# Unread identity products on TensorE ahead of expected waits, in a float32 macaron block of six layers

## The chip, the cores and the metric

The kernel runs on one core of a Trainium2 chip. The metric is the device time of one execution in microseconds (us); the time of a kernel is the median of its runs.

## The reference, cut to what is computed

The input x has 8 batches of 512 tokens with 256 features. Six residual layers follow one another, each on the layer-normalised x. All arithmetic is float32.

```
x = x + 0.5 * fp4_ffn(layernorm(x), w_gate, w_up, w_down)        # hidden 704
x = x + retention(layernorm(x), Wv, Wk, bk, Wq, bq, Wo)          # decay 0.99, blocks of 128
x = x + 0.5 * fp4_ffn(layernorm(x), w_gate, w_up, w_down)
x = x + 0.5 * soft_moe(layernorm(x), gamma_x, gamma_slot, slot_embeds, w1, w2)
x = x + causal_attention(layernorm(x), q, k, v, o with LoRA)     # 16 heads of 16
x = x + 0.5 * soft_moe(layernorm(x), the same weights)

fp4_linear(x, w):  round x and w to FP4 in blocks of 16 along the features, then x @ w.T
soft_moe(x):  logits = rms(x) . rms(slot_embeds)                 # 1024 slots
              slots  = softmax over 8 experts, transposed, @ x
              out    = softmax over slots @ (gelu(slots @ w1) @ w2)    # hidden 1024
```

## The kernel before, in words

All weights stay in SBUF. Two batches are in work at a time, and the instructions of all of them are written into one static program, in an order that the build computes. Three lanes offer work: `front` (the first FFN, retention, the second FFN and the dispatch of the first mixture, lines 1322 to 1330), `back` (attention and the dispatch of the second mixture, lines 1332 to 1338) and `experts` (the expert products and the mixing back, lines 934 to 983). A lane is a generator; it yields the PSUM banks and the results that its next step needs. `drive` (line 1283) picks the lane whose step can begin now and that has had the least of TensorE. DVE steps that can be put off (normalising, rounding to FP4) are kept in chains and put in where DVE would stand (`put_off`, `fill`).

What decides is a model of time, the class `Meter` (line 70). Every instruction goes through `emit` (line 125), which finds when it can begin (`begins`, line 113: the engine is free, the operands are written, the bank has been read), adds a price (`cost`, line 163), records the end, and then issues the real instruction at line 149. That is why nearly all rows of the profile bear L149: they are told apart by tile names. The meter prices a float32 product of n columns at 1.67 ns a column, at least 0.107 us, and a transpose of 128 columns at 0.11 us (lines 167 to 179). A DMA is over after 0.1 us for the meter (line 165), and it knows no clock of TensorE.

PSUM is handed out by `take` as three pairs of banks and two single banks. `not_before` tells the meter when a bank was last read.

The steps that the change and the prediction touch, with their tiles:

- `ffn_weights` (line 513): the gate and up weights come by DMA in three parts, DVE rounds each to FP4, TensorE transposes it (`gut`, line 540), ACT copies it to `w_in`.
- `other_weights` (line 544): transposes `tr_wv`, products `wvo` (4 of 256 columns, lines 584 to 592), transposes `dnt` of the down weights, products `lora_q`, `lora_k`, `lora_v`, `lora_o` on small tiles that come by DMA into one buffer each, transposes `se` of the slot embeddings.
- `ffn` (line 660): for each of four token tiles a transpose `tr_f` of the rounded rows, two times four products `gu_f` of 352 columns, silu and product to `h_f`, rounding, six transposes `hTp_f`, six products `dn_f`.
- `retention` (line 736): transposes `tr_r`, products `k_r`, `q_r`, `v_r`, `a_r` and `y_r`.
- `dispatch` (line 813): transposes `tr_m`, logits `lt_m`, transposes `sm_m`, `l_m` and `nm_m` around the two softmaxes, slots `sl_m` and their transposes `slT_m`.
- `experts`: products `h_e`, `p_e` and `mo_e`.
- `attention` (line 992): `qk_a`, `s_a`, `mx_a`, `st_a`, `c_a`, `ct_a`, `o_a`.

Of the kernel before, what the change touches and what calls it, by code (L numbers as in the profile page):

```python
# [69 lines left out]
class Meter:  # L70
# [2 lines left out]

    LOADS = {AF.Exp: "exp", AF.Gelu: "gelu", AF.Silu: "silu", AF.Sigmoid: "sigmoid"}
    HOP = 0.12
    HOLE = 0.3

    def __init__(self, nc):
        self._nc = nc
        self.at = dict.fromkeys(("PE", "DVE", "ACT", "POOL", "SP"), 0.0)  # L80
        self._written, self._used = {}, {}
        self._table, self._mode = None, None
        self.end, self.last = 0.0, None

        self.banks = set()

        self.holds = {"DVE": [], "POOL": []}

        self.kept, self.fill = None, None
        self.tensor = _Engine(self, "PE", nc.tensor)  # L90
        self.vector = _Engine(self, "DVE", nc.vector)
        self.scalar = _Engine(self, "ACT", nc.scalar)
        self.gpsimd = _Engine(self, "POOL", nc.gpsimd)
        self.sync = _Engine(self, "SP", nc.sync)
# [18 lines left out]
    def begins(self, engine, aps):  # L113

        at = self.at[engine]
        for x in aps:
            for k in self._pieces(x):
                who, t = self._written.get(k, (engine, 0.0))
                at = max(at, t if who == engine else t + self.HOP)
        for k in self._pieces(aps[0]):  # L120
            who, t = self._used.get(k, (engine, 0.0))
            at = max(at, t if who == engine else t + self.HOP)
        return at

    def emit(self, engine, op, call, args, kwargs):
        aps = [x for x in (*args, *kwargs.values()) if isinstance(x, bass.AP)]
        if engine == "DVE" and self.fill:

            while self.begins(engine, aps) > self.at[engine] + self.HOLE and self.fill():
                pass  # L130
        at, cost = self.begins(engine, aps), self.cost(engine, op, args, kwargs, aps)
        if self.shares(engine, op, aps):

            other = self.holds["POOL" if engine == "DVE" else "DVE"]
            for a, b in sorted(other):
                if a < at + cost and at < b:
                    at = b
            other[:] = [x for x in other if x[1] > at - 20.0]
            self.holds[engine].append((at, at + cost))
        at += cost  # L140
        self.at[engine] = self.end = at
        self.last = engine
        for k in self._pieces(aps[0]):
            self._written[k] = (engine, at)
        for x in aps:
            for k in self._pieces(x):
                self._used[k] = (engine, at)
            self._used[x.tensor.name] = at
        call(*args, **kwargs)  # L149

    def shares(self, engine, op, aps):
        if engine == "DVE":
            ins = sum(x.tensor.name not in self.banks for x in aps[1:])
            return ins > 1 or (op == "tensor_scalar" and self.banks.isdisjoint(x.tensor.name for x in aps))
        return engine == "POOL" and len(aps) > 1

    def flush(self):

        kept, self.kept = self.kept, None
        for x in kept or ():  # L160
            self.emit(*x)
# [84 lines left out]
def macaron(ctx: ExitStack, tc: tile.TileContext, a: dict, out: bass.AP):  # L246
    nc = Meter(tc.nc)
# [79 lines left out]

    ident = const.tile([P, P], FP, tag="ident", name="ident")
    make_identity(tc.nc, ident)

    identb = const.tile([P, P], BF, tag="identb", name="identb")
    nc.vector.tensor_copy(identb, ident)
# [3 lines left out]
    for t, step, cm in ((causalb, -1, 1), (causalTb, 1, -1)):  # L336
        nc.gpsimd.memset(t, 0.0)
        nc.gpsimd.affine_select(
            out=t, in_=t, pattern=[[0, 2], [step, P]], compare_op=ALU.is_ge, fill=-1e30, base=0, channel_multiplier=cm
# [851 lines left out]
    def go(lane, chain):  # L1191
# [4 lines left out]
        step()  # L1196
        chain.ready = nc.end + (nc.HOP if nc.last != "DVE" else 0.0)
        if token:
# [47 lines left out]
    def begins(lane):  # L1246
# [8 lines left out]
        for t in lane.needs:  # L1255
            if t not in done:
                return None
            at = max(at, done[t])
        return at + nc.HOP

# [22 lines left out]
    def drive(until=lambda: False):  # L1283
        while not until():
            live = [lane for lane in lanes if advance(lane)]
            if not live and not any(lane.later for lane in lanes):
                break
            least = min((lane.spent for lane in live), default=0.0)
            for lane in lanes:
                lane.spent = max(lane.spent, least - 30.0) if lane in live else max(lane.spent, least)  # L1290
            now = nc.at["PE"]
            if nc.at["DVE"] <= now + 0.5:
                found = put_off(max(now, nc.at["DVE"]))
                if found:
                    go(*found)
                    continue
            when = {lane.name: begins(lane) for lane in live}
            able = [lane for lane in live if when[lane.name] is not None]
            ready = [lane for lane in able if when[lane.name] <= now + SLACK]
            if ready:  # L1300
                emit(min(ready, key=lambda lane: lane.spent))
                continue
            first = min((when[lane.name] for lane in able), default=float("inf"))
            found = put_off(max(nc.at["DVE"], min(first, min(
                (c.ready for lane in lanes for c in lane.later), default=first))))
            if found and not (able and first <= nc.at["DVE"]):
                go(*found)
            else:
                assert able, [(lane.name, lane.banks, lane.needs) for lane in live]
                emit(min(able, key=lambda lane: when[lane.name]))  # L1310
# [94 lines left out]
```

## Time and profile before

| what | value |
|---|---|
| median of 3 runs | 3105.65 us (3105.08 to 10973.31) |
| profiled execution, its own time | 3104.87 us |
| span from first to last instruction | 3103.0 us |
| mean granted clock of TensorE | 0.985 |
| DVE busy | 1558.1 us (50%) |
| ACT busy | 1122.1 us (36%) |
| chain that ended last | PE 90%, DVE 6%, ACT 3%, issue 1% |

The span is what the profile shows; the execution's own time is 1.9 us longer, and its median neighbour another 0.8 us. "PE" is TensorE's matmuls (a transpose is one too), "PEld" its weight loads, which run beside the matmuls. A row of the timeline gives a start, the time from there to the end of the last of the merged instructions, the tiles and the number of records; in brackets stands the time that the engine sat idle before it and who ended that. Since matmuls are pipelined, the pace of a group is read from its start to the start of the next group, not from the duration of one.

### The profile page before, as it was taken

How to read it: one execution, taken by the hardware profiler on the slowest of the kernel's cores; microseconds unless marked ns; L12 is line 12 of the kernel's file. 1: busy time of each engine (PE TensorE's matmuls, PEld its weight loads, DVE VectorE, ACT ScalarE, POOL GpSimd, SP SyncE). 2: the span in 40 equal slices, each digit the busy share in tenths (PEclk: the TensorE clock that was granted, in tenths of full speed). 3: DMA queues.
4: the chain of work that ended last, by engine and by line, in shares of the span. 5: the costliest groups of instructions: out<-in, count | busy, mean ns of one | idle time of the engine just before them, and what ended most of it. 6: DMA issues, size and time to landing. Idle time of an engine off the chain costs nothing.

```text
span 3103.0 us, 36791 instructions
## 1 busy us (share of the span) xinstructions
PE 2948.5 (95%) x15342; PEld 2165.9 (70%) x15342; DVE 1558.1 (50%) x3533; ACT 1122.1 (36%) x1429; POOL 130.0 (4%) x231
## 2 busy tenths in 40 slices
PE   3778899999999999999999999999999999999999
PEld 2455677667776668666786677766777666776778
DVE  6775663645455454635646347354555543424240
ACT  2222352434424334434334343342442433443421
POOL 0000000000000000000000000000000000000000
PEclk8889999999999999999999999999999999999999
DMA  3000000000000000000000000000000000000000
GB/s 123 4 1 1 1 1 1 1 1 1 1 1 1 14 1 1 1 1 15 1 1 1 1 14 1 1 1 1 14 1 1 1 8 1 1 1 1 8 8 7
DMA packets 16806, 18.42 MB, mean 6 GB/s; under 512 B 2048, under 2 KB 16128, under 8 KB 16640
## 3 DMA queue, kind: packets, MB, share of 16 engines
q1 hardware_dynamic: 16640, 16.07, 1.6%
q8 instruction: 121, 1.98, 0.3%
q14 instruction: 45, 0.37, 0.0%
HBM read 11.87 MB, written 4.19 MB: 5 GB/s over the span
## 4 chain that ended last, share of the span: by engine, by line
PE 90%; DVE 6%; ACT 3%; issue 1%; DMA 0%; POOL 0%; SPq 0%; ACTq 0%; POOLq 0%; DVEq 0%
PE p_e L149 14%; PE h_e L149 14%; PE gu_f L149 10%; PE sl_m L149 7%; PE lt_m L149 7%; PE mo_e L149 7%; PE dn_f L149 5%; PE st_a L149 4%; PE s_a L149 4%; PE c_a L149 2%; PE qk_a L149 2%; PE l_m L149 1%; PE hTp_f L149 1%; PE a_r L149 1%; PE y_r L149 1%; PE k_r L149 1%
## 5 line engine op out<-in xcount | busy, mean ns | idle before, releaser
L149 PE MATMUL h_e<-slT_m,w1g 128*128 128x256 f32 x2048 | 463.5, 380 | 2.7 <-ACT pT_a L149 2.5
L149 PE MATMUL p_e<-w,hid_e 128*128 128x256 f32 x2048 | 456.5, 381 | 0.9 <-DVE x L149 0.9
L149 PEld LDWEIGHTS p_e<-w,hid_e 128*128 128x128 f32 x2048 | 388.0, 191 | 58.4 <-issue 4.6
L149 PEld LDWEIGHTS h_e<-slT_m,w1g 128*128 128x128 f32 x2048 | 381.7, 190 | 55.8 <-ACT pT_a L149 3.2
L149 PE MATMUL gu_f<-w_in,y_ffn 128*128 128x352 f32 x1024 | 333.3, 478 | 13.8 <-ACT y_ffn L149 8.3
L149 ACT ACT_TABLE_LOAD x222 | 284.8, 1283 | 109.9 <-PE h_e L149 59.1
L149 DVE TENSOR_REDUCE nmx<-s_a 128x2 f32<-128x256 f32 (+3 forms) x256 | 195.9, 818 | 187.3 <-PE s_a L149 187.0
L149 PEld LDWEIGHTS gu_f<-w_in,y_ffn 128*128 128x128 f32 x1024 | 198.4, 197 | 127.4 <-issue 18.8
L149 ACT ACTIVATE pT_a<-st_a 128x1024 f32<-128x1024 f32 (+1 forms) x192 | 158.8, 879 | 214.4 <-PE st_a L149 214.0
L149 PE MATMUL mo_e<-proc_e,lg_m 128*128 128x257 f32 x1024 | 233.2, 381 | 2.0 <-DVE x L149 1.7
L149 PE MATMUL sl_m<-y_dis,ed_m 128*128 128x257 f32 x1024 | 234.8, 383 | 0.0
L149 PE MATMUL lt_m<-yT_m,seT 128*128 128x512 f32 x512 | 231.5, 599 | 1.7 <-ACT yT_m L149 1.2
L149 ACT ACTIVATE hid_e<-h_e 128x1024 f32<-128x1024 f32 x128 | 131.1, 1024 | 242.2 <-PE h_e L149 241.9
L149 PEld LDWEIGHTS mo_e<-proc_e,lg_m 128*128 128x128 f32 x1024 | 190.5, 189 | 32.2 <-DVE x L149 2.9
L149 PEld LDWEIGHTS sl_m<-y_dis,ed_m 128*128 128x128 f32 x1024 | 192.9, 192 | 28.7 <-issue 1.9
L149 DVE TENSOR_SCALAR_CACHE_REDUCE lg_m<-lt_m 128x512 f32<-128x512 f32 x128 | 84.8, 688 | 222.1 <-PE lt_m L149 222.1
L149 PE MATMUL dn_f<-w_dn,hT_f 128*128 128x256 f32 x768 | 177.1, 383 | 0.0
L149 PEld LDWEIGHTS lt_m<-yT_m,seT 128*128 128x128 f32 x512 | 96.1, 192 | 105.5 <-issue 99.1
L149 ACT COPY proc_e<-p_e 128x512 f32<-128x512 f32 x64 | 37.6, 587 | 359.5 <-PE p_e L149 359.5
L149 PEld LDWEIGHTS dn_f<-w_dn,hT_f 128*128 128x128 f32 x768 | 143.8, 192 | 20.6 <-issue 2.8
L149 ACT ACTIVATE h_f<-gu_f 128x352 f32<-128x352 f32 x128 | 59.3, 464 | 271.6 <-PE gu_f L149 271.3
L149 DVE TENSOR_TENSOR h_f<-h_f,gu_f 128x352 f32<-128x352 f32 x128 | 66.5, 520 | 177.2 <-ACT h_f L149 176.9
(197 smaller groups left out, 3474.4 us busy)
## 6 DMA issues: line engine op xcount, KB each, us to landing
x<-in_L_attn_x SPq DMA_DIRECT2D x8, 512.0 KB, 4.1
out<-x SPq DMA_DIRECT2D x8, 512.0 KB, 3.0
w1g<-in_L_ffn_w SPq DMA_DIRECT2D x1, 1024.0 KB, 5.1
se<-in_L_ffn_slot_embeds SPq DMA_DIRECT2D x1, 1024.0 KB, 7.6
w<-in_L_ffn_w SPq DMA_DIRECT2D x1, 1024.0 KB, 10.1
dn<-in_L_ffn_w_down SPq DMA_DIRECT2D x1, 704.0 KB, 9.5
gu<-in_L_ffn_w_gate SPq DMA_DIRECT2D x1, 640.0 KB, 4.9
gu<-in_L_ffn_w_up SPq DMA_DIRECT2D x1, 640.0 KB, 7.0
```

Source lines behind the costliest of these rows:

```text
L149: call(*args, **kwargs)
```

## The change: what it does

In `emit`, just before a TensorE instruction is accounted for, a new method `keep_up` compares the time at which the instruction begins by the meter with the time from which TensorE is free and the bank that it writes has been read. If the difference is at least 1.0 us (`STAND`), and the output is two-dimensional with 128 partitions, it issues float32 products of the 128x128 identity with itself into the first up to 128 columns of that output. Their number is the difference less 0.3 us, divided by 0.11 us, or by 0.3 us as long as TensorE has had nothing to do by the meter. They are issued on the engine directly, not through the meter, so no other instruction's time in the meter changes. The instruction that follows writes the same columns anew. `macaron` hands the identity to the meter once it is made.

```
     HOP = 0.12
+    STAND = 1.0
     HOLE = 0.3
...
+        self.ident = None
...
         at, cost = self.begins(engine, aps), self.cost(engine, op, args, kwargs, aps)
+        if engine == "PE":
+            self.keep_up(at, aps[0])
...
+    def keep_up(self, until, out):
+        since = max([self.at["PE"]] + [self._used.get(k, (None, 0.0))[1] + self.HOP for k in self._pieces(out)])
+        if self.ident is None or until - since < self.STAND or len(out.shape) != 2 or out.shape[0] != 128:
+            return
+        n = min(128, out.shape[1])
+        took = 0.11 if self.at["PE"] else 0.3
+        for _ in range(int((until - since - 0.3 * self.STAND) / took)):
+            self._nc.tensor.matmul(out[:, :n], self.ident, self.ident[:, :n], start=True, stop=True)
...
     make_identity(tc.nc, ident)
+    nc.ident = ident
```

In the program that results, the order on DVE, ACT, POOL and the DMA queues is that of before, and so is the order of the old instructions on TensorE. TensorE gets 923 more products of 128 columns, in 26 runs. Where they stand (the tile of the instruction that follows, and how many products):

| TensorE's next instruction | products |
|---|---|
| `gut`, three parts | 33, 67, 52 |
| `wvo` | 8 |
| `tr_f`, first batch, first FFN, tile 0 | 79 |
| `dnt`, before its first and its second transpose | 38, 20 |
| `se` | 30 |
| `tr_f`, tiles 2 and 3; `hTp_f`, tile 3 | 64, 28, 36 |
| `tr_f`, second batch; `k_r`, first batch | 35, 6 |
| `tr_f`, first batch, second FFN; `hTp_f`, second batch, tile 3 | 72, 33 |
| `tr_r` and `k_r`, second batch | 28, 8 |
| `tr_m`, before its first and its fourth transpose; `lt_m` | 8, 68, 8 |
| `nm_m`, first batch; `hTp_f`, second batch, second FFN, tile 3 | 61, 46 |
| `gu_f` of batches 3, 5 and 7 | 17, 17, 17 |
| `nm_m` of the last mixture | 44 |

## The prediction

> **What bounds the kernel now.** I read the page first (shares, and the row of slices with the granted clock), then the stretches of the span with their clock, then the waits of PE, then PE's timeline over the first 366 us.
>
> ```profile
> span 3103.0 us, 36791 instructions
> PE 2948.5 (95%) x15342; PEld 2165.9 (70%) x15342; DVE 1558.1 (50%) x3533; ACT 1122.1 (36%) x1429; POOL 130.0 (4%) x231
> PE   3778899999999999999999999999999999999999
> PEclk8889999999999999999999999999999999999999
> ```
>
> ```profile
> 0.00:366.00 366.00, 265.92 (x980) 182.01 (x981) 248.72 (x571) 96.31 (x163) 24.51 (x48) 0.88 0.09 27
> 366.00:3103.00 2737.00, 2682.60 (x14364) 1983.88 (x14362) 1309.38 (x2962) 1025.79 (x1267) 105.48 (x184) 1.00 0.01 3
> 106.00:112.00 6.00, 5.00 (x10) 2.88 (x11) 3.78 (x12) 0.37 (x1) 0.70 (x1) 0.50 0.01 1
> ```
>
> The columns are length, then PE, PEld, DVE, ACT and POOL busy, then the clock. From 366 us on PE is busy 98% at full clock, so whatever makes PE late at 366 us makes the end late by as much. Only the first 366 us hold what the change aims at: 100 us without work on PE, and half clock in places. The 1.00 shown for the first slices is no proof of a full clock there: the `gut` transposes at 14 us have records of 421 ns, against 273 later.
>
> ```profile
> PE tr_f L149 <- DVE y_ffn L149: 26.6, 10, 7.6
> ```
>
> ```profile
> 22.55 1.97 PE L149 MATMUL gut<-ident,gu 128*128 128x128 f32 x8 [6.44 <-DVE gu L149]
> 32.41 3.78 PE L149 MATMUL wvo<-Wo,WvT 128*128 128x256 f32 x8 [0.68 <-ACT WvT L149]
> 43.77 0.66 PE L149 MATMUL tr_f<-ident,y_ffn 128*128 128x128 f32 x2 [7.58 <-DVE y_ffn L149]
> ```
>
> ```profile
> 94.58 0.66 PE L149 MATMUL tr_f<-ident,y_ffn 128*128 128x128 f32 x2 [7.84 <-DVE scale_h_f L149]
> 107.66 7.39 PE L149 MATMUL gu_f<-w_in,y_ffn 128*128 128x352 f32 x16 [0.51 <-ACT y_ffn L149]
> 115.55 2.76 PE L149 MATMUL dn_f<-w_dn,hT_f 128*128 128x256 f32 x12
> 118.14 0.82 PE L149 MATMUL hTp_f<-ident,h_f 128*128 128x128 f32 x6
> 118.80 2.75 PE L149 MATMUL dn_f<-w_dn,hT_f 128*128 128x256 f32 x12
> 162.79 1.47 PE L149 MATMUL a_r<-qT_r,kT_r 128*128 128x256 f32 x8
> 164.10 2.53 PE L149 MATMUL gu_f<-w_in,y_ffn 128*128 128x352 f32 x8
> 180.72 0.66 PE L149 MATMUL tr_f<-ident,y_ffn 128*128 128x128 f32 x2 [6.76 <-DVE y_ffn L149]
> 294.76 4.90 PE L149 MATMUL gu_f<-w_in,y_ffn 128*128 128x352 f32 x16
> ```
>
> ```profile
> L149 PE MATMUL a_r<-qT_r,kT_r x8: 272/327/382, 162.8 to 164.0; 128*128 128x256 f32 x4, 128*128 128x128 f32 x4
> ```
>
> The reader is to see two things. The same 16 records of `gu_f` take 4.90 us at full clock and 7.39 after a stand of PE. And a float32 product makes two records (`wvo` is 4 products in the code and x8 here), a transpose one.
>
> **What one added product costs.** The group `a_r` starts at 162.79 and the next at 164.10: 1.31 us for four records of 256 columns and four of 128. A record of 256 takes 0.216 (twelve `dn_f` from 115.55 to 118.14). That leaves 1.31 - 4 x 0.216 = 0.45 us for four of 128, 0.111 each, weight load beside it. So an unread product, two such records, takes 0.222 us. The upper end is 0.444, at half clock. The lower end is the pace of a transpose, six `hTp_f` in 0.66 us, 0.110. I take 0.222, since `a_r` is the same operation in the same size. The change reckons with 0.11, so each run lasts about twice the stand that it was meant to fill, and TensorE works in order: the real instruction waits behind it.
>
> The Trainium skill, "Perfetto Trace Analysis", section Engine Utilization, halves TensorE's rate for FP32_LOW_HIGH, which by my estimate would be 0.107 us for 128 columns. The trace says 0.222; by the page's figure the change would end near 3083 us.
>
> **Run by run.** Products x 0.222, less the stand that the trace shows there, in us:
> - `gut` first part: 33, free from the identity (1.3 us) on; even with some 12 at half clock they end near 11, before the data at 14.16. Cost 0.
> - `gut` second and third part: 67 and 52, 14.9 and 11.5 against 6.44 and 4.83: +8.4, +6.7. `wvo` 8: 1.8 - 0.7 = +1.1.
> - `tr_f` 79: 17.5 - 7.6 = +10.0. `dnt` 38 and 20: 12.9 - 6.1 = +6.8. `se` 30, no stand: +6.7.
> - `tr_f` 64 and 28: +6.4, +2.7. `hTp_f` 36: +4.8. `tr_f` 35: +4.6. `k_r` 6: +0.5. `tr_f` 72: 16.0 - 6.8 = +9.2. `hTp_f` 33: +4.2.
> - `tr_r` 28: +3.8. `k_r` 8: +0.7. `tr_m` 76: 16.9 - 5.8 = +11.1. `lt_m` 8: +0.6. `nm_m` 61: 13.5 - 5.3 = +8.2. `hTp_f` 46: +7.0.
> - After 366 us: `gu_f` three times 17, 3.8 against 1.0 each: +8.3. Last `nm_m` 44: 9.8 - 3.8 = +6.0.
>
> The sum is 890 x 0.222 - 79.9 = +117.7 us. Every run outlasts its stand, so PE does not stand there any more, and whether DVE's data then come as before or later does not matter. What DVE and ACT wait for behind them (the eviction of `wvo`, at 36.22 before; the silu behind `gu_f`) comes later with PE, never more than PE. No DMA queue is moved past; only the `lora` loads, in single buffers that the product before frees, shift along, with their 6 us of waiting.
>
> **What the clock gives back.** Excess of slow groups over the same group at full clock: six pairs of `gu_f` in the front (8.03, 7.56, 6.53, 7.39, 7.33, 7.82 against 4.90) 15.3; `k_r` 6.46 against 3.70: 2.8; `lt_m` 2.5; `sl_m` 1.6; `dn_f` 2.1; `hTp_f` 1.2; the weights' transposes and `wvo` (`gut`, `tr_wv`, `dnt`, `se`) 6.6; the four `lora` groups 4.1 (2.04 each against an estimated 1.03, from 0.216 a record); the small `tr_f`, `tr_m`, `nm_m` 2.6. Sum 38.8, plus 1.5 at the last `nm_m`: 40. The bounds are 0 (the products do not hold the clock) and these 40; I take 40, because 3 to 6 us of dense products raised the clock in every case shown. [...]
>
> **Sum.** 3104.87 (the profiled execution, 0.8 below the median) + 117.7 - 40 = 3182.5; I say 3183, against the median +77, or 2.5%.
>
> **Rivals.**
> 1. The other side: a product costs as a transpose does, 0.110. Then the runs outlast their stands by 20 us only (mostly at `se`, `gut` and `tr_m`), the clock gives 40, and the end is 3085. It decides below 0.135 us a product, where overrun and gain are equal. For it: both write 128 float32 columns from the identity. Against it: two records a product everywhere else. Chance 0.06.
> 2. Lateness is taken up: PE late by some 64 us at 366 lets DVE and ACT run ahead, and the stands that no product fills shrink: 14 us of them before 366, 6 of these on DMA, and 54 after. That gives 3140 to 3167. Against it: the order on DVE is fixed and interleaved with what PE makes, and the stands after 366 are 1.5 us and less but for one, each behind something that PE made just before. Chance 0.15.
> 3. The clock is not won, or only in part: the `lora` stretch stays slow, a product between identities does not hold the clock. Then 3196 to 3223. For it: the `lora` stretch waits on DMA. Against it: they are matmuls like others to the trace. Chance 0.13.
>
> **How the numbers follow.** The forecast, 3168 to 3196, has 0.66, and 3183 is its time. The range 3155 to 3205 takes in nearly half of rivals 2 and 3, and leaves out the far ends and rival 1, two in ten. A measurement of this kernel can tell about 2%, 62 us, from no change. Slower by more is the forecast and rival 3, 0.79; within it are rivals 2 and 1, 0.20; faster by over 62 us is beyond even the whole gain of clock and stands together, 0.01.
>
> **What would show it.** Each added product as two records, 1846 in all, 0.11 us apart; PE without idle time from 15 us to the first `gu_f` but for `wvo` and `tr_f` behind ACT; `gu_f` at 4.9 us everywhere; clock 1.00 from about 5 us on; the first 366 us of before ending near 430; everything after at the same pace, with +2.8 at each of three `gu_f`. Wrong it would be if the products have one record each, if the first `tr_f` starts before 60 us instead of near 64, or if the late part is shorter than before.

## The result, and the profile after

The changed kernel takes 3186.6 us (median of 6 runs, 3184.1 to 3189.3) against 3105.9 before; the ratio is 1.026, with a 95% interval from 1.025 to 1.028. The forecast was 3183 in a range from 3155 to 3205. The profiled execution took 3188.9 us, with a span of 3186.9. One of the six runs of before took 10973 us; without it their median is 3105.65.

The page of the changed kernel, the rows that were shown of before:

```profile
span 3186.9 us, 40479 instructions
PE 3120.8 (98%) x17188; PEld 2357.3 (74%) x17188; DVE 1558.4 (49%) x3533; ACT 1122.0 (35%) x1429; POOL 130.0 (4%) x231
PE   9899999999999999999999999999999999999999
PEclk9899999999999999999999999999999999999999
```

PE is busier by 172 us and the kernel is 81 us slower: that an engine is busy does not say that its work is of use. The count of PE's records grew from 15342 to 17188, by 1846, twice 923. DVE, ACT and POOL did what they did before.

PE's timeline of the changed kernel. The unread products have line L170 and only the identity as source, the real instructions L153:

```profile
14.79 15.13 PE L170 MATMUL gut<-ident 128*128 128x128 f32 x134
29.75 1.04 PE L153 MATMUL gut<-ident,gu 128*128 128x128 f32 x8
...
46.84 17.80 PE L170 MATMUL tr_f<-ident 128*128 128x128 f32 x158
64.49 0.38 PE L153 MATMUL tr_f<-ident,y_ffn 128*128 128x128 f32 x2
65.37 5.00 PE L153 MATMUL gu_f<-w_in,y_ffn 128*128 128x352 f32 x16 [0.51 <-ACT y_ffn L153]
...
87.82 2.04 PE L153 MATMUL lora_k<-lb_k,la_k 16*128 16x256 f32 x4 [2.13 <-DMA lb_k<-in_L_attn_bk]
98.43 5.06 PE L153 MATMUL gu_f<-w_in,y_ffn 128*128 128x352 f32 x8
```

```profile
136.35 6.42 PE L170 MATMUL tr_f<-ident 128*128 128x128 f32 x56
142.61 0.38 PE L153 MATMUL tr_f<-ident,y_ffn 128*128 128x128 f32 x2
143.49 5.00 PE L153 MATMUL gu_f<-w_in,y_ffn 128*128 128x352 f32 x16 [0.51 <-ACT y_ffn L153]
```

The reader is to see three things. The first run of 28 products (second fence) has 56 records and lasts 6.26 us, from 136.35 to 142.61: 0.112 a record, 0.224 a product. The `tr_f` that began at 43.77 before, after a stand of 7.58, now begins at 64.49 with no bracket behind it: it found its data ready, and waited in the queue behind 158 records. And `gu_f` takes 5.00 us each time instead of up to 8.03; only behind the `lora` groups is it still slow (5.06 for 8 records, against 2.53).

Where the time lies, by the first `h_e` and the last `mo_e`, which hold the same place in TensorE's order in both kernels. Only the starts are compared; an `h_e` row with fewer than 32 records is cut off by the end of the window that was asked for. Before:

```profile
363.94 6.42 PE L149 MATMUL h_e<-slT_m,w1g 128*128 128x256 f32 x29
```

```profile
3084.41 14.08 PE L149 MATMUL mo_e<-proc_e,lg_m 128*128 128x257 f32 x64
```

After:

```profile
433.83 7.07 PE L153 MATMUL h_e<-slT_m,w1g 128*128 128x256 f32 x32
```

```profile
3168.34 14.08 PE L153 MATMUL mo_e<-proc_e,lg_m 128*128 128x257 f32 x64
```

The front is later by 69.9 us (433.83 - 363.94), the rest longer by 14.0 (2734.5 against 2720.5). Together 83.9, the whole difference of the two spans.

### The profile page after: what moved, and what is told of

Read it like the earlier page. It is cut to its first block, busy times and chain, and to the rows that moved or that the text cites. A ratio compares the mean times of both kernels' runs of the same rounds, so it can differ in the third digit from the quotient of the medians.

```text
span 3186.9 us, 40479 instructions
## 1 busy us (share of the span) xinstructions
PE 3120.8 (98%) x17188; PEld 2357.3 (74%) x17188; DVE 1558.4 (49%) x3533; ACT 1122.0 (35%) x1429; POOL 130.0 (4%) x231
## 4 chain that ended last, share of the span: by engine, by line
PE 94%; DVE 3%; ACT 2%; issue 0%; DMA 0%; POOL 0%; SPq 0%; ACTq 0%; POOLq 0%
PE p_e L153 14%; PE h_e L153 14%; PE gu_f L153 10%; PE sl_m L153 7%; PE mo_e L153 7%; PE lt_m L153 7%; PE dn_f L153 5%; PE st_a L153 4%; PE s_a L153 4%; PE c_a L153 2%; PE tr_f L170 2%; PE qk_a L153 2%; PE l_m L153 2%; PE hTp_f L153 1%; PE a_r L153 1%; PE y_r L153 1%
## 5 line engine op out<-in xcount | busy, mean ns | idle before, releaser
L153 PE MATMUL h_e<-slT_m,w1g 128*128 128x256 f32 x2048 | 463.5, 380 | 2.7 <-ACT pT_a L153 2.5
L153 PE MATMUL p_e<-w,hid_e 128*128 128x256 f32 x2048 | 456.7, 381 | 0.9 <-DVE x L153 0.9
L153 PEld LDWEIGHTS p_e<-w,hid_e 128*128 128x128 f32 x2048 | 388.1, 191 | 58.5 <-issue 4.6
L153 PEld LDWEIGHTS h_e<-slT_m,w1g 128*128 128x128 f32 x2048 | 381.7, 190 | 55.8 <-ACT pT_a L153 3.2
L153 PE MATMUL gu_f<-w_in,y_ffn 128*128 128x352 f32 x1024 | 321.4, 465 | 10.6 <-ACT y_ffn L153 5.2
L153 DVE TENSOR_REDUCE nmx<-s_a 128x2 f32<-128x256 f32 (+3 forms) x256 | 196.0, 818 | 188.2 <-PE s_a L153 187.9
L153 PEld LDWEIGHTS gu_f<-w_in,y_ffn 128*128 128x128 f32 x1024 | 192.4, 191 | 116.7 <-issue 9.3
L153 PE MATMUL mo_e<-proc_e,lg_m 128*128 128x257 f32 x1024 | 233.2, 381 | 2.0 <-DVE x L153 1.7
L153 ACT ACTIVATE pT_a<-st_a 128x1024 f32<-128x1024 f32 (+1 forms) x192 | 158.8, 879 | 214.4 <-PE st_a L153 214.1
L153 PE MATMUL sl_m<-y_dis,ed_m 128*128 128x257 f32 x1024 | 232.0, 380 | 0.0
L153 PE MATMUL lt_m<-yT_m,seT 128*128 128x512 f32 x512 | 229.0, 594 | 0.6
L153 ACT ACTIVATE hid_e<-h_e 128x1024 f32<-128x1024 f32 x128 | 131.1, 1024 | 242.2 <-PE h_e L153 241.8
L153 PEld LDWEIGHTS mo_e<-proc_e,lg_m 128*128 128x128 f32 x1024 | 190.6, 190 | 32.2 <-DVE x L153 2.9
L153 PEld LDWEIGHTS sl_m<-y_dis,ed_m 128*128 128x128 f32 x1024 | 190.7, 190 | 28.0 <-issue 1.9
L153 DVE TENSOR_SCALAR_CACHE_REDUCE lg_m<-lt_m 128x512 f32<-128x512 f32 x128 | 84.9, 688 | 230.3 <-PE lt_m L153 230.3
L153 PE MATMUL dn_f<-w_dn,hT_f 128*128 128x256 f32 x768 | 175.1, 379 | 0.0
L153 PEld LDWEIGHTS lt_m<-yT_m,seT 128*128 128x128 f32 x512 | 95.1, 190 | 102.5 <-issue 97.6
L153 DVE TENSOR_TENSOR h_f<-h_f,gu_f 128x352 f32<-128x352 f32 x128 | 66.5, 520 | 207.2 <-ACT h_f L153 206.9
L153 ACT COPY proc_e<-p_e 128x512 f32<-128x512 f32 x64 | 37.6, 587 | 359.8 <-PE p_e L153 359.8
L153 PEld LDWEIGHTS dn_f<-w_dn,hT_f 128*128 128x128 f32 x768 | 142.1, 190 | 20.0 <-issue 2.8
L153 ACT ACTIVATE h_f<-gu_f 128x352 f32<-128x352 f32 x128 | 59.3, 464 | 275.8 <-PE gu_f L153 275.5
```

## The experiments

Each is an edit of the changed kernel, told against before, whose median in their company was 3105.6 to 3105.7 us.

**The right price.** Nothing but the price of a product is set to what the trace shows, which about halves the number. In the trace 936 records are added, 468 products, where 461 were expected.

```
-        took = 0.11 if self.at["PE"] else 0.3
+        took = 0.222 if self.at["PE"] else 0.3
```

> The number of unread products is taken with 0.222 us a product instead of 0.11, so 461 are left of 923; nothing else is changed. Theory (each product costs 0.222 us on TensorE, and what a run outlasts its stand makes everything later): run by run against the stands of the trace before, an overrun of 19 us is left, most of it at se, tr_m and nm_m; the clock gives back 33 us as in the changed kernel; 3106 + 19 - 33 = 3092, some 0.45% below before. Rival (the loss does not go with the number of products but with the runs themselves, by the bank that they hold or the queue that they fill): with the same 26 runs more than half of the 81 us stays, over 3146.

Measured: 3086.4 us, ratio 0.994 (0.993 to 0.995). The kernel is 0.6% faster than before, with the same 26 runs: a small difference, but its slowest run took 3088.6 us and the fastest of before 3104.3. From PE's timeline:

```profile
34.41 8.87 PE L170 MATMUL tr_f<-ident 128*128 128x128 f32 x78
43.12 0.38 PE L153 MATMUL tr_f<-ident,y_ffn 128*128 128x128 f32 x2
44.00 5.00 PE L153 MATMUL gu_f<-w_in,y_ffn 128*128 128x352 f32 x16 [0.51 <-ACT y_ffn L153]
```

The `tr_f` that the change had moved from 43.77 to 64.49 is back at 43.12, and `gu_f` keeps the full clock. The rival, that the runs cost by being there, falls. The time is 5.7 us below the 3092 that was expected; which term of that sum was too large was not traced.

**Transposes in place of products.** The number and the places stay; each product becomes a transpose of the identity, which is one record.

```
-            self._nc.tensor.matmul(out[:, :n], self.ident, self.ident[:, :n], start=True, stop=True)
+            self._nc.tensor.transpose(out[:, :n], self.ident, self.ident)
```

> The same 923 instructions at the same places, but as transposes of the identity, one record each, instead of float32 products of two records. Theory (a record of 128 columns takes 0.11 us at full clock, so the plan's 0.11 is then right): overrun 20 us, clock gain 33 us if transposes hold the clock as products do: 3093. If transposes do not hold the clock, each takes 0.21 us as the transposes before 31 us did, the runs outlast their stands as in the changed kernel, and no gain comes: about 3106 + 890 x 0.215 - 80 = 3217. Rival (the loss goes with the number of instructions, not with the columns that they stream): 3187 as in the changed kernel.

Measured: 3088.1 us, ratio 0.994 (0.993 to 0.996), clock 0.996. It is 4.9 us below the expected 3093, near the miss of the price experiment.

```profile
14.04 1.97 PE L153 MATMUL gut<-ident,gu 128*128 128x128 f32 x8 [6.70 <-DVE gu L153]
15.80 9.28 PE L170 MATMUL gut<-ident 128*128 128x128 f32 x67
24.91 1.04 PE L153 MATMUL gut<-ident,gu 128*128 128x128 f32 x8
25.78 5.84 PE L170 MATMUL gut<-ident 128*128 128x128 f32 x52
```

Here 52 instructions are 52 records, in 5.7 us (25.78 to the next `gut` at 31.46), 0.109 each. So 923 instructions are as cheap as the plan took them to be, and the loss goes with the records, not with the instructions. The rows also show the clock: eight `gut` take 1.97 us after a stand of 6.70, and 1.04 after 67 transposes. Up to the first `wvo` at 33.65 us TensorE has run nothing but transposes, and the granted clock is 0.50 from 14 to 18 us and 1.00 from 20 to 32. So these float32 transposes raise the clock and hold it. The Trainium skill, "TensorE: Matmul & The Clock Gate", Part 4, says that the full clock does not engage for transposes; this run shows that it does.

**The late runs alone.** The first 22 runs are left out.

```
+        self.runs += 1
+        if self.runs <= 22:
+            return
```

> Only the last four of the 26 runs are emitted, those after 366 us: three times 17 products before gu_f and 44 before the last nm_m. Theory (lateness of TensorE goes to the end one to one): 3 x 2.8 + 6.0 - 1.5 = +12.8 us, 3119. Rival (later stands take lateness up): under 3109.

Measured: 3116.0 us, ratio 1.003 (1.002 to 1.004). That is 10.3 us, nearer to 12.8 than to the rival's 3.

```profile
364.32 5.99 PE L154 MATMUL h_e<-slT_m,w1g 128*128 128x256 f32 x27
```

```profile
3095.57 14.08 PE L154 MATMUL mo_e<-proc_e,lg_m 128*128 128x257 f32 x64
```

The last slots of the last mixture, behind the fourth run, before and here:

```profile
3011.43 8.32 PE L149 MATMUL sl_m<-y_dis,ed_m 128*128 128x257 f32 x32
```

```profile
3023.80 7.13 PE L154 MATMUL sl_m<-y_dis,ed_m 128*128 128x257 f32 x32
```

From the first `h_e` to the last `mo_e` it is 2731.3 us, 10.8 more than before. When each PE group's start is compared with its start before, the lateness comes in steps: 2.8 us at each of the three `gu_f`, 5.4 at the last `nm_m`, less 1.2 in the `sl_m` shown, which now has the full clock. That is 12.7 us, the expected 12.8, and no work between takes any of it up. One stretch at half clock that before has near 1769 us is not there in this execution: `p_e` and the group ahead of it are 1.7 us shorter (granted clock 0.64 there before, 1.00 here). 12.7 less 1.7 leaves 11.0, near the 10.8.

**Numbers fitted to the stands.** The number of each run is set by hand to the stand that the trace of before shows, divided by 0.222; `lora_k`, `lora_v` and `lora_o` get 10, 7 and 10.

```
+    COUNTS = [46, 32, 25, 3, 34, 17, 10, 0, 31, 16, 14, 14, 3, 30, 14, 7, 4, 4, 21, 5, 23, 14, 4, 4, 4, 16]
+    LORA = {"lora_k": 10, "lora_v": 7, "lora_o": 10}
...
+        for _ in range(self.lora.pop(out.tensor.name[:6], 0)):
+            self._nc.tensor.matmul(out[:, :128], self.ident, self.ident, start=True, stop=True)
...
-        for _ in range(int((until - since - 0.3 * self.STAND) / took)):
+        self.runs += 1
+        for _ in range(self.COUNTS[self.runs - 1]):
```

> The same kind of products, but their numbers are set by hand, run by run, to the stands that the trace of before shows, at 0.222 us a product (none at se; 10, 7 and 10 added before lora_k, lora_v and lora_o, which wait on DMA). Theory (the loss is the overrun alone, and half clock costs the first 366 us some 35 to 40 us that lie on the path): no overrun beyond 3 us, clock 1.00 from 8 us on, 3066 to 3076. Rival (in the first 366 us DVE sets the pace, so a faster TensorE only stands longer): 3100 to 3108.

Measured: 3074.2 us, ratio 0.990 (0.988 to 0.991), clock 0.998. This version beats both kernels, by 1% and by 3.5%.

```profile
40.89 0.44 PE L156 MATMUL tr_f<-ident,y_ffn 128*128 128x128 f32 x2
41.83 5.00 PE L156 MATMUL gu_f<-w_in,y_ffn 128*128 128x352 f32 x16 [0.51 <-ACT y_ffn L156]
...
58.08 1.13 PE L156 MATMUL lora_k<-lb_k,la_k 16*128 16x256 f32 x4
66.29 2.63 PE L156 MATMUL gu_f<-w_in,y_ffn 128*128 128x352 f32 x8
71.34 1.51 PE L156 MATMUL se<-ident,se 128*128 128x128 f32 x8 [2.41 <-issue]
```

```profile
333.03 7.07 PE L156 MATMUL h_e<-slT_m,w1g 128*128 128x256 f32 x32
```

The first `h_e` is 30.9 us earlier than before, and all that is left of the path is 2720.8 us, as before. So the clock's time lay on the path, and DVE did not set the pace of the front. Of the 38.8 us that slow groups had cost, 30.9 came back net; a part of the rest is a new stand, 2.41 us before `se`, where TensorE now is early.

**Products before the loads that it waits on.** The changed kernel, its 923 products kept, with the `LORA` lines of the version above.

> The changed kernel with all its 923 products, and 10, 7 and 10 more before lora_k, lora_v and lora_o, where TensorE waits some 2 us each on DMA. Theory (what the prediction missed is the half clock that stayed there: three lora groups of 2.04 us instead of 1.13, eight records of gu_f of 5.06 instead of 2.53, products before se at half clock): the 27 products fit into the waits, and 6 us come back, 3181 on 3187. Rival (the stretch is bound by the loads, not by the clock): no change, 3187, or later by up to 6 us if the products delay the loads.

Measured: 3184.8 us (3182.3 to 3185.6), ratio 1.025 (1.024 to 1.027).

```profile
88.11 1.13 PE L155 MATMUL lora_k<-lb_k,la_k 16*128 16x256 f32 x4
...
96.32 2.63 PE L155 MATMUL gu_f<-w_in,y_ffn 128*128 128x352 f32 x8
```

```profile
428.91 7.07 PE L155 MATMUL h_e<-slT_m,w1g 128*128 128x256 f32 x32
```

The trace agrees with the theory: `lora_k` takes 1.13 us instead of 2.04, `gu_f` 2.63 instead of 5.06, and the first `h_e` is 4.9 us earlier than in the changed kernel, all of it won by the `se` transposes (at 105.49 instead of 110.40). The times show only 1.8 us between the medians, with overlapping intervals, so as a gain in time this is inconclusive.

**Half-filled stands.** The numbers of the fitted version, halved in every run.

```
-    COUNTS = [46, 32, 25, 3, 34, 17, 10, 0, 31, 16, 14, 14, 3, 30, 14, 7, 4, 4, 21, 5, 23, 14, 4, 4, 4, 16]
-    LORA = {"lora_k": 10, "lora_v": 7, "lora_o": 10}
+    COUNTS = [23, 16, 12, 2, 17, 8, 5, 0, 15, 8, 7, 7, 2, 15, 7, 4, 2, 2, 10, 2, 11, 7, 2, 2, 2, 8]
+    LORA = {"lora_k": 5, "lora_v": 4, "lora_o": 5}
```

> As in the kernel with numbers fitted to the stands, but half as many products in every run (and 5, 4, 5 before the lora groups), so each stand begins with products and ends idle. Theory (the clock falls only after some 3.4 us without work, and the idle ends are under 4 us but for the first, about 8 us): most of the gain stays, 3074 to 3082, clock at least 0.995. Rival (the clock follows the share of time that TensorE works, so half-filled stands lose it): the gain is halved or worse, 3090 to 3106, clock 0.99 or lower.

Measured: 3093.5 us, ratio 0.996 (0.995 to 0.997), clock 0.989. The six runs fall into two groups, three from 3088.1 to 3089.7 us with a clock of 0.989 to 0.991 and three from 3097.2 to 3097.7 with 0.987; the median lies between them, where no run does. My theory was wrong here, and the rival's numbers hold for the median: of the 31 us that the fitted version had gained, about half is gone in the first group and three quarters in the second. The profile is of a run of the first group.

```profile
29.24 1.07 PE L156 MATMUL gut<-ident,gu 128*128 128x128 f32 x6 [2.92 <-DVE gu L156]
30.10 1.06 PE L156 MATMUL tr_wv<-ident,Wv 128*128 128x128 f32 x4
...
88.48 0.69 PE L156 MATMUL tr_f<-ident,y_ffn 128*128 128x128 f32 x2 [3.24 <-DVE y_ffn L156]
89.67 7.44 PE L156 MATMUL gu_f<-w_in,y_ffn 128*128 128x352 f32 x16 [0.51 <-ACT y_ffn L156]
...
101.22 0.44 PE L156 MATMUL tr_f<-ident,y_ffn 128*128 128x128 f32 x2 [1.67 <-DVE y_ffn L156]
102.17 5.00 PE L156 MATMUL gu_f<-w_in,y_ffn 128*128 128x352 f32 x16 [0.51 <-ACT y_ffn L156]
```

Behind idle ends of 2.92 and 3.24 us the clock fell (four `tr_wv` in 1.06 us instead of 0.60, `gu_f` 7.44), behind one of 1.67 it did not. A bound of 3.4 us of idle time, on which my theory stood, is too kind. Nor does the length of the idle time decide alone, as three stands of the same length in the trace of before show:

```profile
124.72 0.87 PE L149 MATMUL hTp_f<-ident,h_f 128*128 128x128 f32 x6 [3.17 <-DVE h_f L149]
205.19 1.54 PE L149 MATMUL hTp_f<-ident,h_f 128*128 128x128 f32 x6 [3.17 <-DVE h_f L149]
351.16 1.30 PE L149 MATMUL hTp_f<-ident,h_f 128*128 128x128 f32 x6 [3.17 <-DVE h_f L149]
```

After the first the clock stays full, after the other two it falls, though each follows over 11 us of nearly unbroken work. Whether the share of work in a longer stretch or the phase of a window decides, these runs do not tell apart.

## Why the prediction was right, step by step

- **A product costs 0.222 us**, two records. Shown: 1846 more records, 0.112 us apart; the transposes show the other price, 0.109, at the same number of instructions. Rival 1 priced this at 3085 us, and the kernel in which each added instruction does cost that took 3088. The other estimate in the prediction, 0.107 us, is close to one record, not to a product.
- **Every run outlasts its stand, +117.7 us.** Shown by the timeline without stands before the filled instructions and by the price experiment. One stand was added that I had not listed: 0.9 us before the 64 products of `tr_f`, at 115.58, where DVE was still reading the bank. And 0.6 us of the stand that I had counted at the second batch's `tr_r` stayed, since the run there stands behind it.
- **The clock gives 40 us back.** The direction is shown, the size was too large, and this is the term that was mis-sized. I took the upper bound, `lora` included. In the changed kernel half clock stayed over that stretch, as rival 3 had it: 0.9 us in each of three groups, 2.5 in `gu_f`, about 0.5 in the products of `se`, 0.3 in `tr_f`, about 6 together; filling that stretch brought 4.9 of it back. With the stands of 0.9 and 0.6 that is about 1 us more than the 5.3 by which the front came out above the sum (69.9 against 103.4 - 38.8 = 64.6). So two of the signs that were named did not come: `gu_f` was not at 4.9 us everywhere, and the clock was not full from 5 us on.
- **Lateness goes to the end one to one.** Shown by the late runs alone and by the same steps in the changed kernel: 2.8 us at each of three `gu_f` and 4.2 at the last `nm_m` and the `sl_m` behind it, 12.7 together against 8.3 + 6.0 - 1.5 = 12.8. So the 1.5 us credited there did come, as 1.2. That the whole late part is +14.0, close to the 14.3 without that credit, is chance: a stretch at half clock near 1385 us, which before does not have there, adds 1.6. Rival 2 falls.
- **The sum** for the profiled execution was 3182.5 against 3188.9. The median lies closer, at 3186.6, since that execution is one of the longer ones; that part of the closeness is luck.

## What to carry to other kernels

Filling TensorE's stands to hold its clock pays, here 1%, but only when a filler is priced by its own records in the trace: a float32 product is two of them, a transpose one. A filler that outlasts its stand is paid in full, because TensorE's next instruction waited behind it in every case here; one that ends well before the stand's end may lose the clock after all. Before filling, add up what the slow groups cost: here 40 us was the whole prize, and any plan with more than that in overrun had to lose, as this one did with 118.

## What was not expected of the hardware

Float32 transposes alone raise TensorE's clock and hold it (granted clock 1.00 from 20 to 32 us, before any product has run). The clock can fall after an idle end of 2.9 us that follows dense products (four `tr_wv` then took 1.06 us instead of 0.60), and three idle stretches of the same 3.17 us ended twice in half clock and once not.
